# One layer block on one core: prologue and seams listed anew, a lead of 80, and the rotations' fourth layer behind the next pair's third

## The chip, the cores and the metric

The kernel runs on one core of one Trainium2 chip. The metric is the device time of one execution in microseconds (us). Engines are named as the profile names them: PE (TensorE, matmuls; PEld its weight loads), DVE (VectorE), ACT (ScalarE), POOL (GpSimd) and SP (SyncE, which here only issues DMAs). Each engine runs its own instructions in order; L633 is line 633 of the kernel before.

## What is computed

The input x is 2 x 2048 tokens of 256 features, in float32. Four residual layers follow each other: x + attention_a(layernorm(x)), x + ffn(layernorm(x)), x + attention_b(layernorm(x)), x + ffn(layernorm(x)), the two ffn with the same weights.

```python
# attention_a: 16 query heads of 16 features, 4 key/value heads, softmax over all 2048 keys
out = softmax(q @ k.T / 4) @ v;  return out @ Wo + bo
# ffn: three cycles over all tokens
gf = sigmoid(g3(gelu(g2(gelu(g1(x.mean(tokens)))))))          # once for each batch
for _ in range(3):
    tf = sigmoid(w4(gelu(w3(gelu(w2(gelu(w1(out))))))))       # layers of 256, 128, 64, 1
    out = out + (0.1 + range * (0.7*gf + 0.3*tf - 0.5) * 2) * twist(out)
# attention_b: linear attention, masked, no softmax: silu(q), silu(k) rotated, gate, norm, Wo
```

## The kernel before, in words

The 4096 tokens stand in SBUF as 8 blocks of 512 (blocks 0 to 3 are batch 0). The program is one list of instructions written by hand: Python generators are stepped at chosen places, and in_order (L136) ties each engine's instructions to the order of that list. So a line's place in the list is its place in the queue of every engine that it uses, SP's among them in the prologue (L627).

**Attention a** has 32 units, one for each block and group of four heads. For each unit, largest (L361) first finds the largest score of every query row: 64 steps of one matmul s (L376) and one DVE reduction (L380) over its 512 columns. After the last step nm (L390) joins them, ACT and POOL split it in two parts mt (L397, L398), and turn_maxima (L400) turns mt on DVE (L403) and sends it through DRAM to a_m with eight small DMAs. For every unit but the first and the last that turn stands behind the fourth step of the next unit (L386). Then the unit's 16 rounds kb (L638) compute the scores a second time, transposed: p is a score matmul (L648) and a matmul that subtracts the maxima (L652); ACT takes the exponential (L656); one round later weigh (L633) multiplies with the values into av. The steps of largest run ahead of the rounds. The prologue (L508 to L627) does LEAD = 74 steps before the first round; each round does four more (L659 to L673), and odd rounds of unit 0 one extra until six are done (L687, MORE), so that from round 11 on the lead is 80.

The prologue's other work is a generator, pieces (L593): block j's normalised tokens are turned (features), its keys and values made (keys, with transfers through DRAM that end in a_kP), its queries made for two halves (asked), its values turned (values). The loop at L623 takes one step and, at chosen n, one piece: 17 pieces at n = 4, 7, ..., 52 and five at n = 64, 66, ..., 72. A second generator, rows (L212), loads Wo and the output bias bo on SP (L216, L217, issued at L584); makes a diagonal matrix a_db of bo on POOL (L221); and multiplies it with ones on PE (a_pb, L226), which DVE copies to a_bo_row (L227). Its second step stands at L606, ahead of block 4's pieces, and its third at L619, behind them. a_bo_row is first read in unit 1 (L467).

**The rotations** (L773) are the ffn. Blocks go in pairs, four pairs by three cycles, so k = 0 to 11. For pair k, first(k, e) is layer 1 of one block (8 matmuls q1f, gelu on ACT to a1), second(k) layer 2 of both (8 matmuls q2f, gelu to a2), third(k) layer 3 of both (q3f, gelu to a3), and fourth(k) layer 4 and the update: two matmuls q4f, tanh on ACT, then for each block two DVE and two POOL multiplications and sums that rewrite zq (L852 to L864). Pair k + 4 reads that zq. In the last cycle (k of 8 and more) fourth is back (L886): the blocks are turned back to tokens on PE (trf) and added to xs by DVE (L879, L912). context (L777) is the gf network of one batch in four steps: gm on DVE (L781), p1f, p2f, p3f on PE with ACT between. fourth needs its result for its batch. rounds(f, n) (L1208) lists the steady part: even n is fourth(k-2), second(k-1), first(k, 0); odd n is third(k-1), first(k, 1), with k = n // 2.

**The seams.** Between the first rotations and attention b (L1300 to L1322) block 0's query, key, gates and values are made while pair 11 ends; each of query and key is a projection on PE, silu on ACT, products on POOL and a shuffle on DVE, and rotate adds the two parts on DVE (L1043). Between attention b and the second rotations (L1391 to L1409) the last block is normalised and turned (next_turn), and context(1) runs step by step (front1).

Of the kernel before, what the change touches and what calls it, by code (L numbers as in the profile page):

```python
# [20 lines left out]
NB = T // BLK  # L21
BPB = N // BLK
KB = N // P
# [44 lines left out]
def tile_hybrid(ctx: ExitStack, tc: tile.TileContext, x: bass.AP, consts: bass.AP, wa_d: bass.AP, wf_d: bass.AP, wb_d: bass.AP, out: bass.AP):  # L68
# [84 lines left out]
    def attention_a():  # L153
        with ExitStack() as st:
# [150 lines left out]
            def keys(j, ld):  # L305

                pk = psp.tile([P, BLK], F32, tag="p", name=f"pk{j}")
                for c in range(2):
                    mm(pk, wkv[:, c, :], planes[j][c], start=(c == 0), stop=(c == 1))
                kv = kvs[j] = ld.tile([P, BLK], F32, tag="kv", name=f"kv{j}")  # L310
                kh, kl = (ld.tile([64, BLK], d, tag=t, name=f"{t}{j}") for t, d in (("kh", F32R), ("kl", F32)))
                if j == 0:
                    halve(kh, kl, None, pk[0:64, :], bkv[0:64, :])
                    nc.scalar.activation(kv[64:P, :], pk[64:P, :], AF.Identity, bias=bkv[64:P, :])
                else:
                    nc.scalar.activation(kv, pk, AF.Identity, bias=bkv)
                    halve(kh, kl, kv[0:64, :], None, None)
                d = stored("dk", (kh, kl), (0, 0, 1, 1), nc.sync)
                return lambda: fetch([kP[p][:, j * BLK : (j + 1) * BLK] for p in range(2)], d)
# [41 lines left out]
            def largest():  # L361


                turning = []
                for u, (j, g) in enumerate(units):
                    k0 = (j // BPB) * N
                    qP = queries[u]
                    mx = sb.tile([P, KV, 4, 4], F32, tag="mx", name=f"mx{u}")
                    first = u == 0

                    def step(kb, qi, r):

                        pool, tag = (psp, "p") if first and (4 * qi + r) % 5 > 2 else (pss, "s")
                        s = pool.tile([P, BLK], F32, tag=tag, name=f"s{u}_{kb}_{qi}_{r}")
                        row = slice(64 * (r % 2), 64 * (r % 2) + 64)
                        mm(  # L376
                            s, qP[r // 2][row, qi * P : (qi + 1) * P],
                            kP[r // 2][row, k0 + kb * BLK : k0 + (kb + 1) * BLK], start=True, stop=True,
                        )
                        nc.vector.tensor_reduce(mx[:, r, qi : qi + 1, kb], s, AX.X, ALU.max)  # L380

                    for kb in range(4):
                        for qi in range(4):
                            for r in (0, 1, 3, 2):
                                step(kb, qi, r)
                                if (kb, qi, r) == (0, 0, 2) and turning:  # L386
                                    turning.pop()()
                                yield
                    nm = sb.tile([P, KV, 4], F32, tag="nm", name=f"nm{u}")
                    nc.vector.tensor_reduce(nm, mx, AX.X, ALU.max, negate=True)  # L390

                    mt = sb.tile([P, KV, 2, 4], F32, tag="mt", name=f"mt{u}")
                    if first:
                        nc.vector.tensor_copy(mt[:, :, 0, :].bitcast(F32R), nm)
                        nc.vector.tensor_tensor(mt[:, :, 1, :], nm, mt[:, :, 0, :], ALU.subtract)
                    else:
                        nc.scalar.copy(mt[:, :, 0, :].bitcast(F32R), nm)  # L397
                        nc.gpsimd.tensor_tensor(mt[:, :, 1, :], nm, mt[:, :, 0, :], ALU.subtract)  # L398

                    def turn_maxima(u=u, mt=mt):  # L400

                        mr = sb.tile([P, 32], F32, tag="mr", name=f"mr{u}")
                        turn = nc.vector.transpose(mr, mt.rearrange("p r i q -> p (r i q)"))  # L403
                        tc.keep_in_program_order(turn)
                        d = dram.tile([2 * KV, BLK], F32, tag="dm", name=f"dm{u}")
                        for i in range(4):
                            nc.sync.dma_start(
                                d.rearrange("r (q b x) -> (r q) b x", b=4, x=32)[:, i, :], mr[32 * i : 32 * i + 32, :]
                            )
                        for p in range(2):  # L410
                            for i in range(2):
                                nc.sync.dma_start(
                                    mrows[u % 2][p][64 * i : 64 * i + 2, :].bitcast(F32),
                                    d[4 * p + 2 * i : 4 * p + 2 * i + 2, :],
                                )

                    if first or u + 1 == len(units):
                        turn_maxima()
                    else:
                        turning.append(turn_maxima)  # L420
# [83 lines left out]
                        nc.vector.tensor_tensor(pair, pair, po.rearrange("p (t d) -> p t d", t=2), ALU.add)  # L504
                        yield


            LEAD, MORE, WARM = 64 + 10, 6, 6  # L508
            ahead = largest()
            begin = len(nc.cur_bb.bb.instructions)  # L510
            loads = ExitStack()
# [47 lines left out]
            second = keys(1, ld)  # L559
# [5 lines left out]
            third = keys(2, ld)  # L565
# [6 lines left out]
            third = keys(3, ld)  # L572
# [10 lines left out]
            more = rows()  # L583
            next(more)  # L584

            def memsets():
                for t in mrows[0] + mrows[1]:
                    nc.gpsimd.memset(t.bitcast(F32), 0.0)
                nc.gpsimd.memset(pick.bitcast(F32), 0.0)
                for p in range(2):  # L590
                    nc.gpsimd.memset(pick[64 * p : 64 * p + 2, :].bitcast(F32), 1.0)

            def pieces():  # L593

                memsets()
                look(4)
                values(3)
                for j in range(1, BPB):
                    for m in range(2):
                        asked(j, m)  # L600
                        yield
                        if (j, m) == (2, 0):
                            spread(4, ld, 0)
                next(more)
                for j in range(BPB, NB):
                    features(j, ld, 0)  # L606
                    if j + 1 < NB:
                        look(j + 1)
                    yield
                    keys(j, ld)()  # L610
                    if j + 1 < NB:
                        spread(j + 1, ld, 0)
                    yield
                    asked(j, 0)
                    yield
                    asked(j, 1)
                    values(j)
                    if j == BPB:
                        next(more)  # L619
                    yield  # L620

            rest = pieces()
            for n in range(4, LEAD):  # L623
                next(ahead)
                if (n % 3 == 1 and n < 55) or (n > 63 and n % 2 == 0):
                    next(rest, None)
            in_order(begin, (engines.DVE, engines.Activation, engines.Pool, engines.SP))  # L627

# [9 lines left out]
            for u, kb in ((u, kb) for u in range(len(units)) for kb in range(KB)):  # L638
# [45 lines left out]
                if kb > 1:  # L684
                    next(done, None)
                    next(norms, None)
                if kb % 2 == 1 and u * KB + kb < 2 * MORE:  # L687
                    next(ahead)
                if u % G == 1 and kb == 1 and G < u < 4 * G:
                    norms = norm(u // G - 1)  # L690
                if kb == 4 and u + 2 < len(units):
# [32 lines left out]
    def behind(tail):  # L724
# [483 lines left out]
        def rounds(f, n):  # L1208

            context, first, second, third, fourth, _ = f  # L1210
            k = n // 2
            if n % 2 == 0:
                if 0 <= k - 2:
                    fourth(k - 2)
                if 0 <= k - 1 < 12:
                    second(k - 1)
                if k < 12:
                    first(k, 0)
            else:
                if 0 <= k - 1:  # L1220
                    third(k - 1)
                if k < 12:
                    first(k, 1)

        f = rotations(0, sums0, False)
        context, first, second, third, fourth, _ = f
# [20 lines left out]
        front, front1, more = context(0), context(1), linear_weights()  # L1247
# [42 lines left out]
        next(front1)  # L1290
        first(4, 0)
        next(front1)
        fourth(2)
        aside = {10: more, 12: more}
        for n in range(9, 22):
            rounds(f, n)
# [3 lines left out]
        zero, one = blocks[0], blocks[1]  # L1300
# [11 lines left out]
        zero.turn()  # L1312
        third(11)
        zero.query()
        zero.rotate()
        zero.key()
        fourth(11, zero.rotate)
        zero.narrow()
        zero.gates()
        zero.keys_by_tokens()  # L1320
# [4 lines left out]
        context, first, second, third, fourth, turn_ahead = f  # L1325
# [70 lines left out]
        second(1)  # L1396
        fourth(0)
        first(2, 1)
        x.next_turn()
        third(1)  # L1400
        next(front1)
        fourth(1)
        next(front1)
        second(2)
        first(3, 0)
        next(front1)
        third(2)
# [9 lines left out]
        in_order(begin)  # L1417

    behind(attention_a())


# [115 lines left out]
```

## Time and profile before

| | |
|---|---|
| median of 3 runs | 2130.35 us (2127.65 to 2135.94) |
| the profiled execution | 2133.95 us, of which the profile's span is 2132.2 |
| prologue | 0 to about 107 us |
| 32 units of attention a | 107 to 1527 |
| first rotations, with the end of attention a | 1527 to 1697 |
| middle seam | 1697 to 1721 |
| attention b, with the start of the second rotations | 1721 to 1976 |
| last seam | 1976 to 2000 |
| second rotations | 2000 to 2132 |

A group's row gives line, engine, operation, output and inputs, count, then busy time, mean of one, and the idle time before with what ended it. The timeline gives start and length in us, and in brackets the idle time before a row and what released it. A row of stretches gives for each engine the busy us and the instructions; then PE's granted clock, where 1.00 is full speed, the share of the DMA engines, and GB/s. In the chain that ended last, a row is start, length and what ran; the whole chain is PE for 93% of the span and DVE for 3%.

### The profile page before, as it was taken

Reading aid. Unit: us, or ns where it says so; the run is one execution under the profiler, and the core shown is the slowest. Engines: PE = TensorE matmul, PEld = TensorE weight load, DVE = VectorE, ACT = ScalarE, POOL = GpSimd, SP = SyncE. Lnnn points to the kernel's source line nnn. Section 1 sums busy time; section 2 is a strip of 40 time slices with the busy share of each in tenths; the row PEclk is TensorE's granted clock in tenths of the full one; section 3 lists DMA queues with packets and bytes.
Section 4 is the critical chain, followed back from the end, with each engine's and each line's share of the span. In section 5 each row is a group of like instructions: output and inputs, shape, how many; then the busy total and the mean of one; then the engine's idle time right before and its main releaser. Section 6 shows DMA issues by size and latency. Waiting matters only on the chain.

```text
span 2132.2 us, 38745 instructions
## 1 busy us (share of the span) xinstructions
PE 2101.0 (99%) x14158; PEld 1018.7 (48%) x14158; DVE 1700.7 (80%) x3241; ACT 1427.6 (67%) x2787; POOL 355.6 (17%) x352
## 2 busy tenths in 40 slices
PE   9899999999999999999999999999999999999998
PEld 4344444444444444444444444444443567776434
DVE  7689998998999999899899899987134688886335
ACT  4377777777777877777777777777864445554443
POOL 3100000001001000000000000000135355551450
PEclk9799999999999999999999999999999999999999
DMA  6320110101101011010110101100100000000002
GB/s 204 92 88 10 49 37 17 47 10 47 37 19 37 18 49 39 18 38 20 47 37 20 37 19 48 38 18 8 52 1 1 0 2 1 2 1 2 0 0 79
DMA packets 59695, 68.71 MB, mean 32 GB/s; under 512 B 24944, under 2 KB 34032, under 8 KB 59248
## 3 DMA queue, kind: packets, MB, share of 16 engines
q1 hardware_dynamic: 58592, 64.79, 11.2%
q8 instruction: 111, 1.82, 0.4%
q10 hardware_dynamic: 720, 0.92, 0.1%
q14 instruction: 80, 0.66, 0.1%
q0 software_dynamic: 192, 0.52, 0.1%
HBM read 35.78 MB, written 26.21 MB: 29 GB/s over the span
## 4 chain that ended last, share of the span: by engine, by line
PE 93%; DVE 3%; issue 1%; ACT 1%; POOL 1%; DMA 1%; SPq 0%; DVEq 0%; POOLq 0%; ACTq 0%
PE av L633 24%; PE s L376 22%; PE p L648 11%; PE q1f L817 8%; PE p L652 7%; PE q2f L827 4%; PE pe L1117 2%; PE bpo L1143 2%; PE po L499 1%; PE pq L975 1%; PE pk L975 1%; PE pw L984 1%; PE pv L984 1%; DVE mx L380 1%; PE q3f L839 1%
## 5 line engine op out<-in xcount | busy, mean ns | idle before, releaser
L380 DVE TENSOR_REDUCE mx<-s 128x1 f32<-128x512 f32 x2048 | 1272.7, 683 | 110.7 <-PE s L376 106.4
L656 ACT ACTIVATE e<-p 128x512 f32<-128x512 f32 x2048 | 1057.7, 603 | 312.8 <-PE p L652 305.9
L376 PE MATMUL s<-a_kP,qP 64*128 64x512 f32 x2048 | 707.0, 471 | 4.8 <-DVE mx L380 2.8
L652 PE MATMUL p<-a_m,a_pick 64*128 64x512 f32 x2048 | 586.5, 415 | 0.0
L376 PEld LDWEIGHTS s<-a_kP,qP 64*128 64x128 f32 x2048 | 283.5, 184 | 567.4 <-DVE mx L380 550.8
L633 PE MATMUL av<-e,a_v 128*32 128x512 f32 x4096 | 546.8, 605 | 0.0
L648 PE MATMUL p<-qP,a_kP 64*128 64x512 f32 x2048 | 527.5, 394 | 2.5 <-ACT e L656 2.5
L648 PEld LDWEIGHTS p<-qP,a_kP 64*128 64x128 f32 x2048 | 286.9, 185 | 64.6 <-ACT e L656 25.5
L652 PEld LDWEIGHTS p<-a_m,a_pick 64*128 64x128 f32 x2048 | 284.6, 184 | 26.1
L817 PE MATMUL q1f<-zq,wf 128*128 128x512 f32 x384 | 175.7, 600 | 0.0
L633 PEld LDWEIGHTS av<-e,a_v 128*32 128x32 f32 x4096 | 81.0, 108 | 129.2 <-issue 121.2
L818 ACT ACTIVATE a1f<-q1f,wf 128x512 f32<-128x512 f32 x96 | 65.8, 686 | 102.2 <-PE q1f L817 99.0
L398 POOL TENSOR_TENSOR mt<-nm,mt 128x16 f32<-128x16 f32 x31 | 6.9, 221 | 736.3 <-ACT mt L397 736.3
L817 PEld LDWEIGHTS q1f<-zq,wf 128*128 128x128 f32 x384 | 70.5, 190 | 97.4 <-issue 84.9
L827 PE MATMUL q2f<-a1f,wf 128*128 128x512 f32 x192 | 90.7, 616 | 0.0
L1123 DVE TENSOR_TENSOR en<-pe,small 128x512 f32<-128x512 f32 x128 | 79.4, 683 | 11.3 <-PE pe L1117 11.2
L237 POOL TENSOR_TENSOR ql<-zq,qh 128x512 f32<-128x512 f32 x15 | 19.3, 1286 | 359.5 <-ACT qh L234 359.5
L858 DVE TENSOR_SCALAR cf<-cf,f_beta,alphaf 128x512 f32<-128x512 f32 x32 | 33.6, 1050 | 54.0 <-ACT cf L857 54.0
L862 POOL TENSOR_TENSOR tf<-cf,zq 128x512 f32<-128x512 f32 x32 | 56.6, 1768 | 93.5 <-DVE cf L858 93.1
L829 ACT ACTIVATE a2f<-q2f,wf 128x512 f32<-128x512 f32 x48 | 32.6, 685 | 53.3 <-PE q2f L827 53.3
L827 PEld LDWEIGHTS q2f<-a1f,wf 128*128 128x128 f32 x192 | 35.6, 195 | 45.8 <-issue 44.7
L864 POOL TENSOR_TENSOR zq<-zq,tf 128x512 f32<-128x512 f32 x32 | 56.8, 1776 | 2.5
(209 smaller groups left out, 1633.5 us busy)
## 6 DMA issues: line engine op xcount, KB each, us to landing
qP<-dq SPq DMA_DIRECT2D x64, 256.0 KB
dq<-qh SPq DMA_DIRECT2D x62, 128.0 KB
dq<-ql SPq DMA_DIRECT2D x62, 128.0 KB
a_kP<-dk SPq DMA_DIRECT2D x16, 256.0 KB
oc<-avs SPq DMA_DIRECT2D x128, 32.0 KB
sums<-dr SPq DMA_DIRECT2D x128, 32.0 KB
out<-xs SPq DMA_DIRECT2D x16, 256.0 KB
xs<-in_x SPq DMA_DIRECT2D x7, 512.0 KB
```

The costliest lines, as they stand in the source:

```text
L376: mm(s, qP[r // 2][row, qi * P : (qi + 1) * P], kP[r // 2][row, k0 + kb * BLK : k0 + (kb + 1) * BLK], start=True, stop=True,)
L380: nc.vector.tensor_reduce(mx[:, r, qi : qi + 1, kb], s, AX.X, ALU.max)
L633: mm(av[32 * r : 32 * r + 32, :], vA[:, units[u][0] // BPB * KB + kb, 32 * r : 32 * r + 32], es[r], start=(kb == 0), stop=(kb == KB - 1),)
L648: mm(t[r], kP[r // 2][row, k0 : k0 + P], qP[r // 2][row, :], start=True, stop=False)
L652: mm(t[r], pick[row, :], mrow[r // 2][row, :], start=False, stop=True)
L656: nc.scalar.activation(es[r], t[r], AF.Exp, scale=1.0 / HD**0.5)
L817: mm(q1, w1[:, c, m * P : (m + 1) * P], z[:, c, :], start=(c == 0), stop=(c == 1))
L818: nc.scalar.activation(a1[:, m, :], q1, AF.Gelu, bias=b1[:, m : m + 1])
L827: mm(q2, w2[:, c, :], a1[:, c, :], start=(c == 0), stop=(c == 1))
L862: nc.gpsimd.tensor_tensor(t1, cs, z[:, 0, :], ALU.mult)
L864: nc.gpsimd.tensor_tensor(z[:, 1, :], z[:, 1, :], t1, ALU.subtract)
L1123: nc.vector.tensor_tensor(self.ens[t][w], pes[w].rearrange("p (h n) -> p h n", h=4), const("triu").unsqueeze(1).to_broadcast([P, 4, P]), A ...
```

## The change

LEAD becomes 80, and the extra steps of unit 0 (MORE) go. The prologue's 22 pieces are spread anew: 19 at n = 4, 7, ..., 58 and three at n = 64, 66, 69; ten steps then stand alone. Both remaining steps of rows go into the last piece. The turn of a unit's maxima stands one reduction earlier. In rounds, and where the seams are written out, fourth(k) of the first two cycles stands behind third(k + 1) and not ahead of second(k + 1). In the middle seam block 0's key is projected between the two halves of fourth(11). In the last seam second(2) stands ahead of fourth(1), and next_turn behind third(1).

```diff
-                                if (kb, qi, r) == (0, 0, 2) and turning:
+                                if (kb, qi, r) == (0, 0, 3) and turning:
...
-            LEAD, MORE, WARM = 64 + 10, 6, 6
+            LEAD, WARM = 64 + 16, 6
...
-                next(more)
                 for j in range(BPB, NB):
                     features(j, ld, 0)
...
-                    if j == BPB:
+                    if j + 1 == NB:
+                        next(more)
                         next(more)
...
-                if (n % 3 == 1 and n < 55) or (n > 63 and n % 2 == 0):
+                if n % 3 == 1 and n < 61 or n in (64, 66, 69):
                     next(rest, None)
...
-                if kb % 2 == 1 and u * KB + kb < 2 * MORE:
-                    next(ahead)
...
-                if 0 <= k - 2:
+                if 0 <= k - 2 and k - 2 >= 8:
                     fourth(k - 2)
...
                     third(k - 1)
+                if 0 <= k - 2 < 8:
+                    fourth(k - 2)
...
         next(front1)
-        fourth(2)
         aside = {10: more, 12: more}
...
         zero.query()
+        def amid():
+            zero.rotate()
+            zero.key()
+        fourth(11, amid)
         zero.rotate()
-        zero.key()
-        fourth(11, zero.rotate)
...
         first(2, 1)
+        third(1)
         x.next_turn()
-        third(1)
         next(front1)
+        second(2)
         fourth(1)
         next(front1)
-        second(2)
         first(3, 0)
```

## The prediction

> **What bounds the kernel now.** I read the page first, then busy time by stage, the timelines of three places where TensorE (PE) stands still, and the chain that ended last. The page:
>
> ```profile
> PE 2101.0 (99%) x14158; PEld 1018.7 (48%) x14158; DVE 1700.7 (80%) x3241; ACT 1427.6 (67%) x2787; POOL 355.6 (17%) x352
> ...
> PEclk9799999999999999999999999999999999999999
> ```
>
> PE is the bound nearly everywhere; the digits of its granted clock name one place where it is not simply busy, slice 2 (53 to 107 us). By stage (columns: stretch, length, then busy us of PE, PEld, DVE, ACT, POOL, then the clock):
>
> ```profile
> 0.00:107.00 107.00, 94.84 (x290) 42.02 (x292) 72.26 (x182) 39.30 (x75) 28.78 (x49) 0.87 0.51 148
> 152.00:198.00 46.00, 46.00 (x344) 20.61 (x340) 42.74 (x72) 35.83 (x71) 0.22 (x1) 1.00 0.07 20
> 1600.00:1697.00 97.00, 97.00 (x298) 43.71 (x297) 51.15 (x120) 44.47 (x70) 45.24 (x33) 1.00 0.00 1
> 1697.00:1721.00 24.00, 20.66 (x118) 13.02 (x116) 21.83 (x56) 11.99 (x23) 10.40 (x8) 1.00 0.00 1
> 1976.00:2000.00 24.00, 21.24 (x56) 9.26 (x55) 12.86 (x26) 11.29 (x22) 14.08 (x10) 0.86 0.00 0
> ```
>
> The attention loop (152 to 198) and the rotations (1600 to 1697) are full: only shorter PE work helps there. Prologue, middle seam (1697 to 1721) and last seam (1976 to 2000) have idle PE, and two of them a lower clock.
>
> **The bias block.** Line 606 makes bo_row inside the prologue. Timeline of before:
>
> ```profile
> 54.61 0.46 PE L326 MATMUL pv<-small,kv 64*128 64x64 f32 x4
> 57.90 0.42 SPq L217 DMA_DIRECT2D a_bo<-in_wa  x1
> 59.62 0.76 POOL L221 TENSOR_TENSOR a_db<-small,a_bo 128x128 f32<-128x128 f32 x2 [23.14 <-DMA a_bo<-in_wa]
> 60.43 1.22 PE L226 MATMUL a_pb<-a_db,small 128*128 128x256 f32 x2 [5.37 <-POOL a_db L221]
> 61.69 0.42 DVE L227 COPY a_bo_row<-a_pb 128x256 f32<-128x256 f32 x1 [6.93 <-PE a_pb L226]
> ```
>
> POOL waits 23.14 us for the load of bo, at the end of SP's queue; PE waits 5.37 for POOL, DVE 6.93 for PE. Behind POOL's wait also stand kl (61.58) and the statistics of block 5. Then the clock:
>
> ```profile
> 56.00:58.00 2.00, 0.00 (x0) 0.00 (x0) 0.00 (x0) 0.00 (x0) 0.00 (x0) 0.76 0.41 119
> 70.00:72.00 2.00, 2.00 (x6) 0.59 (x5) 0.18 (x1) 0.96 (x2) 0.00 (x0) 0.83 0.00 0
> 86.00:88.00 2.00, 0.61 (x5) 0.27 (x4) 2.00 (x5) 0.00 (x0) 0.00 (x0) 0.94 0.32 36
> 100.00:102.00 2.00, 2.00 (x5) 0.36 (x3) 0.00 (x0) 0.61 (x1) 0.00 (x0) 0.65 0.00 0
> ```
>
> Full speed is 1.00 and the low state 0.50, so the means give the edges: half clock from 57.04 to 70.68 and from 87.76 to 101.40, 13.64 us each. The first follows the idle stretch; the second follows twelve reductions in a row (from 82.4) in which PE only trickles. In them four matmuls take 3.60 to 3.78 us instead of 1.98.
>
> **Prologue after, step by step.** The block goes to the last piece, where bo is long there. From 55.07 on nothing then waits, and pieces and steps go on as just before: one cycle of a block (12 steps, four pieces) took 45.43 to 55.7, that is 10.3 us (DVE: 12 reductions of 0.62, a look of 2.0, a cast 0.4). Blocks 5 and 6 end at 76.3. Turning block 7 and the six steps to n = 64 are DVE's: 3.6, to 79.9. Then PE's pk 1.98, two pq 3.96, values 0.46, pb 0.6 (half of 1.22, at full clock) and five scores 1.2: 88.1. Ten steps are left plus the loop's first ones; DVE paces them at 0.62, and the first p (L648) starts with reduction 78 at 94.4. Before it started at 106.99. Lower bound: DVE alone from 54.76, 48 reductions 29.8, looks 4.4, casts 1.3, maxima 0.8, copy 0.4: 91.5. Upper bound: one more spell of half clock over these 8.2 us of PE work: 100.5. What is late next is DVE. SP's queue keeps its order: the keys' transfers of block 4 still start at 58.43 and take some 5.4 us a block (two issues 1.1 ahead of kl, 62.87 to 67.14 behind it), but they feed only the second batch, units 16 on. POOL has the sums for bo (0.76) at about 86, behind kl of block 7, and nothing waits there.
>
> **Lead of 80.** The six extra steps at odd kb (L687) leave the loop. There av starts at 111.66 for kb 1 and 143.06 for kb 11, 3.14 us a round; in the full stage 181.50, 184.21, 186.91, 2.705 a round. After: av of kb 1 at 94.4 + 4.4, of kb 11 27.05 later: 125.9 against 143.1, **17.2 us** for both together. But the ten bare steps (PE 0.22 of each 0.62) are like those before 87.76, so I expect half clock at the loop's start: 2 us lost (bounds 0 and 6.8, half of 13.64). Net **-15.2**, from -8 to -18.
>
> [...]
>
> **Turn of the maxima one reduction earlier** (L386). nm ends 0.75 us before mt is ready (188.26 to 189.01); the transpose now comes 2.1 after nm instead of 2.6. DVE still doesn't wait. Its eight DMAs come 0.6 earlier on an SP queue with nothing else to issue then, and nothing waited for a_m. 0 (bounds -0.2 and +0.2 in each of 31 units).
>
> **Fourth behind third** (L1210, 11 rounds). One round of before, and one behind transposes, in the chain:
>
> ```profile
> 1638.39 3.63 PE q2f L827 x8
> 1642.03 3.43 PE q1f L817 x8
> 1646.47 3.63 PE q1f L817 x8
> 1651.16 3.63 PE q2f L827 x8
> ...
> 1665.45 3.44 PE q2f L827 x8
> ```
>
> Round 12.77 = 3.63 + 3.43 + 1.0 (q3) + 3.63 + 1.06 (q4). Eight matmuls behind the narrow q3 or q4 take 0.2 more than behind full ones (3.44). With q4 behind q3 one such change goes: 0.2 x 11 = **-2.2** (bound 0, if q3 to q4 costs as much). Cover: q2's second half needs a1 0.69 after PE and has 1.7 of its first half. The new z is needed after first 3.6, second 3.4, first 3.4, q3 and q4 2.1, first 3.6 and second 3.4, 19.5 us, and takes 10 (two ACT 1.3, a DVE 0.6, POOL 4 x 1.77, gaps 1); no wait. At the start of the first rotations fourth(2) only changes places with q3.
>
> **Middle seam.** The key's projection moves between the halves of fourth(11). DVE works the same list (swaps, 3.74 twice, rotations) with the second 3.74 ahead of the key's rotation instead of behind; PE waited there for DVE (pv 1.47, pt 0.72). rotk, at 1717.3 before, comes at 1716.9 to 1717.9. 0, bounds -1.7 and +3.7.
>
> **Last seam.** Timeline of before:
>
> ```profile
> 1990.00 1.13 PE L852 MATMUL q4f<-a3f,wf 64*128 64x512 f32 x4 [0.79 <-ACT a3f L841]
> 1991.82 0.15 DVE L781 TENSOR_REDUCE gmf<-sums 128x2 f32<-128x8 f32 x1
> 1993.10 1.01 PE L786 MATMUL p1f<-gmf,wf 128*128 128x1 f32 x4 [1.97 <-DVE gmf L782]
> 1993.98 6.28 PE L827 MATMUL q2f<-a1f,wf 128*128 128x512 f32 x8
> ```
>
> gm stands in DVE's queue behind fourth(0), which waits for POOL; PE idles 0.79 and 1.97, the clock falls (1992.4 to 1999.2) and q2 takes 6.28. After, second(2) comes before fourth(1): from 1987.17 q3 1.0, turn 1.0, q2 3.5, q4 1.06, p1 0.4 end at 1994.1; gm (1993.05) is there at 1993.7. first(3, 0) starts at 1994.1 instead of 2000.09: **-5.9** (bounds -2.8, the two waits alone, and -6.5). PE is full from there to 2116, so it stays.
>
> **Sum.** -15.2 - 2.2 - 5.9 = -23.3. The profiled execution took 2133.95 (span 2132.2 and 1.75 around it): 2110.6. The median shown, 2130.35, lies 3.6 lower, so **2107**.
>
> **Rivals.** (A) The forecast, 2107 (2100 to 2112): chance 0.55. (B) The half clock lasts four windows as at 57 and 87, at the loop's start (6.8 instead of 2) or over block 7's pieces (6): 2112, both 2118; for it the two rows, against it the loop, which once lost the clock, at 333, and had it back 3.4 us later; 0.22. (C) The wait for bo was hiding another, so that prologue and loop start give half, 8: 2114, and without the last seam 2120; for it the crowded DMA (share 0.51), against it that everything loaded by 57 is read after it; 0.18, half of it above 2119.7. (D) Slower: the transpose, now after three reductions, waits for POOL in each unit. It decides from mt later than 2.1 us after nm (0.75 seen); with POOL's bias add of 2.4 ahead of it, 3.15, DVE stops 1.05 x 31 = 33 us: 2140. Against it: that add follows mt (146.50 after 146.32); 0.05.
>
> About 0.5% (10.7 us) is what a measurement can tell from no change. Faster 0.55 + 0.22 + 0.09 = 0.86, within 0.09, slower 0.05. Range 2100 to 2120: A, B and most of C.
>
> **What would show it.** Right: no PE gap at 55 to 60, clock 1.00 until about 91, first L648 at 94.4, av every 2.7 from kb 1, q2 at 3.44 in the rotations, no p1 wait. Wrong: L648 after 100, a transpose waiting for POOL, or q1f waiting for zq.

## The result, and the profile after

| | median us | executions |
|---|---|---|
| before | 2132.62 | 4 (2127.65 to 2135.94) |
| changed | 2108.61 | 4 (2107.98 to 2109.11) |

The ratio is 0.9889 (95%: 0.9867 to 0.9911): 24.0 us less, where 23.3 were forecast (2107, 2100 to 2120). The profiled execution took 2107.98, of which its span is 2106.2; so 26.0 us lie between the two spans. The page of the changed kernel:

```profile
PE 2085.9 (99%) x14158; PEld 1011.4 (48%) x14158; DVE 1697.6 (81%) x3241; ACT 1427.5 (68%) x2787; POOL 355.2 (17%) x352
...
PEclk9999999999999999999999999999999999999999
```

PE does the same 14158 matmuls in 15.1 us less, and the 7 in the clock's digits is gone. Busy time by stage (prologue to the first p, middle seam, last seam up to first(3, 0)):

```profile
0.00:94.07 94.07, 89.27 (x297) 39.39 (x297) 75.57 (x189) 39.80 (x76) 28.81 (x49) 0.99 0.60 174
1679.00:1703.00 24.00, 21.20 (x113) 13.22 (x113) 19.80 (x57) 12.44 (x24) 9.96 (x8) 1.00 0.00 1
1956.00:1974.73 18.73, 18.73 (x58) 7.91 (x57) 8.57 (x20) 11.12 (x21) 8.35 (x7) 1.00 0.00 0
```

The prologue's clock went from 0.87 to 0.99, the last seam is full at 1.00, and the middle seam still has 2.8 us of idle PE. The bias block and the first p in the timeline (what is line 648 before is 647 here; later lines shift by two or three):

```profile
84.71 0.75 POOL L221 TENSOR_TENSOR a_db<-small,a_bo 128x128 f32<-128x128 f32 x2
87.38 0.70 PE L226 MATMUL a_pb<-a_db,small 128*128 128x256 f32 x2
88.11 0.42 DVE L227 COPY a_bo_row<-a_pb 128x256 f32<-128x256 f32 x1 [1.52 <-PE a_pb L226]
...
94.07 1.22 PE L647 MATMUL p<-qP,a_kP 64*128 64x512 f32 x2
```

POOL's wait of 23.14 and PE's of 5.37 are gone, and no wait of that kind took their place (DVE waits 1.52 for a_pb): the first p starts at 94.07 instead of 106.99. The clock, by stretches of 2 us:

```profile
90.00:92.00 2.00, 1.80 (x4) 0.71 (x4) 2.00 (x4) 0.00 (x0) 0.00 (x0) 0.82 0.23 44
96.00:98.00 2.00, 2.00 (x12) 1.16 (x10) 1.83 (x4) 1.52 (x3) 0.00 (x0) 0.50 0.95 364
98.00:100.00 2.00, 2.00 (x17) 0.73 (x13) 1.94 (x4) 1.82 (x4) 0.00 (x0) 0.97 0.66 273
```

By the same reading as in the prediction, one spell of half clock is left, from 91.28 to 98.12 (6.84 us), where there were two of 13.64. It begins in the bare steps, and DVE is nearly full in it (1.80 or more of each 2.00). A round of the rotations, in the chain that ended last:

```profile
1613.94 1.06 PE q4f L849 x4
1615.00 3.63 PE q1f L814 x8
1618.63 3.43 PE q2f L824 x8
```

q2 now takes 3.43 behind q1 instead of 3.63 behind q4; a round takes 12.56 (q4 at 1601.38, 1613.94 and 1626.51) where it took 12.77. The last seam in the timeline:

```profile
1972.29 0.15 DVE L778 TENSOR_REDUCE gmf<-sums 128x2 f32<-128x8 f32 x1
1973.20 1.13 PE L849 MATMUL q4f<-a3f,wf 64*128 64x512 f32 x4
1974.26 0.61 PE L783 MATMUL p1f<-gmf,wf 128*128 128x1 f32 x4
1974.73 3.68 PE L814 MATMUL q1f<-zq,wf 128*128 128x512 f32 x8
```

gm is ready while q4 runs, so p1 has no wait for DVE (1.97 before), and the clock holds. first(3, 0) starts at 1974.73 instead of 2000.09.

The whole path between the two traces, by how much earlier the same instruction comes in the changed kernel: 17.0 at the av of round 11 (126.09 for 143.06) and 17.45 some units later; 18.9 behind 337, because the profiled execution of before lost the clock at 333 and that of the changed kernel did not; 18.2 at the end of attention a; then 0.7 in the first rotations, 0.65 in the middle seam, 5.84 in the last seam and 0.6 in the second rotations. The sum is 26.0.

### The profile page after: what moved, and what is told of

It reads as the page before. It is cut to its first block, busy times and chain, and to the rows that moved or that the text cites. A ratio compares the mean times of both kernels' runs of the same rounds, so it can differ in the third digit from the quotient of the medians.

```text
span 2106.2 us, 38754 instructions
## 1 busy us (share of the span) xinstructions
PE 2085.9 (99%) x14158; PEld 1011.4 (48%) x14158; DVE 1697.6 (81%) x3241; ACT 1427.5 (68%) x2787; POOL 355.2 (17%) x352
## 4 chain that ended last, share of the span: by engine, by line
PE 95%; DVE 2%; DMA 1%; ACT 1%; issue 0%; POOL 0%; SPq 0%; DVEq 0%; ACTq 0%; POOLq 0%
PE av L632 24%; PE s L376 23%; PE p L647 12%; PE q1f L814 8%; PE p L651 7%; PE q2f L824 4%; PE pe L1114 2%; PE bpo L1140 2%; PE po L499 1%; PE pq L972 1%; PE pw L981 1%; PE pv L981 1%; PE pk L972 1%; PE q3f L836 1%; PE pq L336 1%; DVE mx L380 1%
## 5 line engine op out<-in xcount | busy, mean ns | idle before, releaser
L491 POOL TENSOR_TENSOR oc<-oc,sums 128x512 f32<-128x512 f32 x16 | 20.6, 1288 | 209.6 <-DMA sums<-dr 138.2
```

## The experiments

The experiments come in three groups, each with its own executions of the kernel before: medians 2130.12 (e1 to e4), 2130.41 (e5 to e8) and 2132.84 (e9 to e12). Ratios are to these. "After" is the changed kernel.

**e1: after, with the bias block back in its two old places.**

```diff
+                next(more)
                 for j in range(BPB, NB):
...
-                    if j + 1 == NB:
-                        next(more)
+                    if j == BPB:
                         next(more)
```

> The changed kernel with the bias block alone put back to where it stood, ahead of and behind block 4's pieces. If the wait for bo and the half clock behind it cost about 10 us in the prologue (my theory), the first shifted score comes near 104 instead of 94.1, PE stands idle some 5 us near 55 again, and the time is about 2118. If the lead and the new spacing made the gain and the wait hid something else (rival), it stays below 2112.

2118.33 us, ratio 0.9946 (0.9927 to 0.9965); first p at 104.36. The wait is back, in the timeline of e1:

```profile
61.34 0.75 POOL L221 TENSOR_TENSOR a_db<-small,a_bo 128x128 f32<-128x128 f32 x2 [23.67 <-DMA a_bo<-in_wa]
```

So 11.8 us of the gain are left without the block's move, and by the medians 12.4 of the 24.2 that e5 shows hang on it. By the traces it is less: av of round 11 comes at 136.44 in e1 and at 126.09 in after, 10.35 later, and the distance is 10.3 at the end too.

**e2: before, with the block alone moved to the last piece** (the same lines, the other way round).

> The kernel before with the bias block alone moved to the last piece. My theory: the first shifted score at about 97 instead of 107, time some 10 us below the kernel before (near 2122). Rival (the wait hid another): not more than 3 us below it.

2118.70, ratio 0.9949 (0.9933 to 0.9964): 11.4 less, more than expected, with the first p at 93.53. In its trace the bare steps at the end of the old spacing cost less clock than they did in before. Stretches of e2:

```profile
78.00:80.00 2.00, 1.90 (x5) 0.82 (x6) 2.00 (x4) 0.00 (x0) 0.00 (x0) 0.72 0.81 260
82.00:84.00 2.00, 2.00 (x12) 1.13 (x12) 1.06 (x3) 0.95 (x2) 0.00 (x0) 0.92 0.05 6
```

Half clock from 78.88 to 82.32: one stretch of 3.4 us, where before had 13.64 behind the same twelve reductions.

**e3: before, with bo loaded early on ACT's queue and the block left in its place.**

```diff
-                nc.sync.dma_start(bo, wa_d[:, slice(*_WA["bo"])])
...
+            nc.scalar.dma_start(bo, wa_d[:, slice(*_WA["bo"])])
```

> The kernel before with the bias block in its old place, but bo loaded at the start from ACT's queue. If only the lateness of the load was the trouble, this is as fast as moving the block, near 2122 with the first shifted score at about 97. If the place itself costs (POOL, PE and DVE in one chain amid the pieces), the gain is under half of that, above 2127.

2121.19 (2116.10 to 2124.38), ratio 0.9958 (0.9942 to 0.9974); profiled at 2116.85, with a_pb at 56.28 without a wait and the first p at 93.64. In these traces the place was not the trouble, the late load was: either cure brings the first p to 93.6. But the executions fall into two groups: 2116.1 and 2116.9 at a mean clock of 0.997, and 2120.3 to 2124.4 at 0.994 to 0.995. The trace is of the faster group, and e2 has no such slower group; whether the block in its old place costs clock in the others is open.

**e4: before, with idle matmuls on PE ahead of a_pb**, to tell the half clock behind the wait from the wait itself.

```diff
+                warm = psp.tile([P, BLK], F32, tag="p", name="warm")
+                for _ in range(6):
+                    mm(warm, still[:, 0:P], still, start=True, stop=True)
                 pb = psp.tile([P, BLK], F32, tag="p", name="a_pb")
```

> The kernel before with twelve idle matmuls (5.1 us, their result unused) ahead of the bias block's on PE: the wait stays, but PE is not idle in it. If the half clock behind the wait costs by itself (my theory: 4 to 5 of the 10 us), the clock stays at 1.00 from 55 to about 85, and the time is near 2127. If what counts is the wait alone, the time stays at 2131 or more although the clock stays up.

2131.01, ratio 1.0002 (0.9991 to 1.0013). In its trace the clock is 1.00 from 54 to 84, and the way from a_pb to the score of step 40 takes 6.92 (62.07 to 68.99) instead of 10.85 (60.43 to 71.28), so there the half clock behind the wait cost 3.9. (The idle matmuls themselves hold a_pb up by 1.1: a_db is done at 60.94.) The first p comes at 101.05, 5.9 us earlier, also because the spell of half clock at the bare steps lasts 6.8 there and not 13.64. But that execution took 2127.24, near the lowest of the ten (2125.84 to 2134.31), and the median gains nothing: that the half clock behind the wait costs 4 to 5 us by itself is not borne out by the times. What the other executions lost instead can't be read from one trace; this stays open.

**e5 and e12: after again**, as marks for the others.

> The changed kernel once more, as the mark for the three beside it: 2108.6 by its first runs (2108 to 2109).

> The changed kernel again, as the mark for the other three: the time of e5, within 1 us (2105 to 2107.5).

2106.24 (2104.85 to 2108.32), ratio 0.9886 (0.9871 to 0.9900), and 2108.33 (2108.22 to 2109.45), ratio 0.9887 (0.9870 to 0.9904): within 2.1 us of each other on different chips, 24.2 and 24.5 below their own before.

**e6: after, with the last seam as before.**

```diff
         first(2, 1)
-        third(1)
         x.next_turn()
+        third(1)
         next(front1)
-        second(2)
         fourth(1)
         next(front1)
+        second(2)
```

> The changed kernel with the last seam alone as it was. My theory (gm behind fourth(0) stops PE, and the clock falls): 5.8 us slower than the changed kernel, near 2114.4, with half clock for some 3.4 to 6.8 us in the seam. [...] Rival (PE only waits somewhere else): within 1 us of it.

2111.99, ratio 0.9913 (0.9898 to 0.9928): 5.75 slower than e5. Timeline of e6:

```profile
1973.66 0.88 PE L783 MATMUL p1f<-gmf,wf 128*128 128x1 f32 x4 [1.97 <-DVE gmf L779]
1974.40 5.09 PE L824 MATMUL q2f<-a1f,wf 128*128 128x512 f32 x8
```

The wait of 1.97 returns to the hundredth, and with it a loss of the clock: q2 takes 5.09 instead of 3.60. But not all of the 5.75 is the seam. In its trace e6 is 1.54 behind e5 where first(2, 1) begins, part of it through half clock in the middle seam (1697.4 to 1700.8), which the edit doesn't touch, and 6.06 behind at first(3, 0): 4.5 for the seam. The other traces with the old seam say why that is less than the 5.84 between before and after. In e3 the clock stays at 1.00 through it, with the same wait in front of p1:

```profile
1979.38 3.68 PE L827 MATMUL q2f<-a1f,wf 128*128 128x512 f32 x8
```

From first(2, 1) to first(3, 0) it takes 13.46 there; 15.16 in e2 and 15.14 in e6, with 3.4 of half clock; 16.35 in e4 and 16.46 in before, with 6.8; and 10.63 in the new order. So the two waits cost 2.8, the first 3.4 us of half clock 1.7 more and the next 3.4 another 1.2 to 1.3, and how much of it comes differs between executions of the same seam.

**e7: after, with the fourth layer ahead of the second again, in rounds and at the start of the first rotations.**

```diff
-                if 0 <= k - 2 and k - 2 >= 8:
+                if 0 <= k - 2:
...
-                if 0 <= k - 2 < 8:
-                    fourth(k - 2)
...
         next(front1)
+        fourth(2)
```

> The changed kernel with fourth ahead of second again in the rounds, the seams as changed. My theory (0.2 us for each change between narrow and full matmuls): rounds of 12.77 instead of 12.57, 1.5 to 2.2 us slower in all, near 2110.4. Rival (the order does nothing for PE): within 0.5 us.

2108.35, ratio 0.9894 (0.9879 to 0.9908): 2.1 slower than e5 by the medians, 2.4 by the spans. The spans hold more than the edit, because e7's profiled execution lost the clock twice in attention a (half clock from 315 to 319 and from 677 to 680). Between the same instructions the first and the second rotations take 0.7 longer each, 1.4 together. The chain of e7 shows the old price:

```profile
1618.70 1.06 PE q4f L849 x4
1619.76 3.63 PE q2f L824 x8
```

**e8: after, with the turn of the maxima behind the fourth reduction again.**

```diff
-                                if (kb, qi, r) == (0, 0, 3) and turning:
+                                if (kb, qi, r) == (0, 0, 2) and turning:
```

> The changed kernel with the turn of the maxima behind the fourth reduction again. The two traces drift apart by 0.03 us a unit against the earlier turn, so by that theory 0.9 us faster, near 2107.7. Rival (the earlier transfers of the maxima help): slower by up to 1 us.

2105.71, ratio 0.9882 (0.9866 to 0.9899): 0.5 faster than e5, which the medians can't tell from nothing. The traces can't either. An nm stands at 213.9 in both, and at the first q3 of the round at 1598 e8 is 0.72 ahead (1598.18 for 1598.90), 0.02 us for each unit; but the same program drifts by more: from the av of round 11 to the last av it takes 1384.98 in after, 1383.50 in e5 and 1385.07 in e12, without half clock in between, 1382.73 in e8, and 1383.49 in e10, which has e8's turn. In the changed kernel PE's next weight load of a score waits for the turn (mr) in each unit, but the same load waits as long in e8, for a reduction. First after, then e8:

```profile
259.68 0.19 PEld L376 LDWEIGHTS s<-a_kP,qP 64*128 64x128 f32 x2 [0.84 <-DVE mr L403]
259.46 0.18 PEld L376 LDWEIGHTS s<-a_kP,qP 64*128 64x128 f32 x2 [0.84 <-DVE mx L380]
```

So no price of the earlier turn is shown.

**e9: after, with the lead and the pieces' spacing as before.**

```diff
-            LEAD, WARM = 64 + 16, 6
+            LEAD, MORE, WARM = 64 + 10, 6, 6
...
-                if n % 3 == 1 and n < 61 or n in (64, 66, 69):
+                if (n % 3 == 1 and n < 55) or (n > 63 and n % 2 == 0):
...
+                if kb % 2 == 1 and u * KB + kb < 2 * MORE:
+                    next(ahead)
```

> The changed kernel with the lead and the spacing of the pieces as before (74 steps and six extra ones in the loop), the bias block still in the last piece. If most of the prologue's gain is the block and the lead adds the rest: first p at about 93.5, as in e2, rounds of 3.14 up to kb 11, so some 5 to 6 us later than the changed kernel from kb 11 on, 2112 (half clock behind the bare steps at the end of the prologue may add or spare 2). If the lead is worth nothing: within 1 us of the changed kernel. If the two parts only work together: above 2116.

2112.57 (2111.30 to 2117.02), ratio 0.9911 (0.9895 to 0.9927): 4.2 slower than e12. Its prologue is that of e2, step for step, but its trace shows another clock. Stretches of e9:

```profile
78.00:80.00 2.00, 1.72 (x4) 0.97 (x5) 2.00 (x5) 0.00 (x0) 0.00 (x0) 0.52 0.81 230
90.00:92.00 2.00, 2.00 (x4) 0.46 (x3) 0.00 (x0) 0.25 (x1) 0.00 (x0) 0.57 0.00 0
```

Half clock from 78.08 to 91.72, 13.64 us, and the first p at 98.19 instead of 93.53. (It also lost the clock at 27 and at 505, for 3.4 us each.) That execution took 2116.27 at a mean clock of 0.994, and one more took 2117.02; the three at 0.997 to 0.998 took 2111.3 to 2112.6. So one list of instructions has two outcomes some 5 us apart; in the traces of e2 and e9 the difference at the first p is whether the clock comes back after one stretch of 3.4 us or after four.

**e10: after, with the last three pieces at n = 63, 68 and 73, and e8's edit**, meant to beat both kernels.

```diff
-                if n % 3 == 1 and n < 61 or n in (64, 66, 69):
+                if n % 3 == 1 and n < 61 or n in (63, 68, 73):
```

> The changed kernel with its last three pieces at n = 63, 68 and 73, so that fewer steps stand bare, and with the turn of the maxima behind the fourth reduction as before. If DVE's idle time of 1.8 in the prologue's end can be filled and the single spell of half clock there goes: 1 to 2 us for the prologue and 0.5 for the turn, 2 us faster than the changed kernel. If DVE's list alone sets the first p: only the 0.5.

2113.62 (2111.07 to 2117.76), ratio 0.9911 (0.9896 to 0.9927): 5.3 slower than e12, with the first p at 98.50. The theory that DVE's list alone sets the first p falls here. Stretches of e10:

```profile
82.00:84.00 2.00, 0.00 (x0) 0.00 (x0) 1.93 (x4) 0.00 (x0) 1.72 (x3) 0.98 0.60 130
86.00:88.00 2.00, 2.00 (x3) 0.76 (x3) 0.60 (x2) 0.00 (x0) 0.00 (x0) 0.50 0.31 103
```

Timeline of e10:

```profile
84.27 1.39 PE L376 MATMUL s<-a_kP,qP 64*128 64x512 f32 x2 [3.16 <-DVE mx L380]
```

Behind step 64 DVE joins and turns the maxima of the first unit (nm, mt and mr, 81.59 to 83.64). With the piece moved from n = 64 to 63 PE has nothing to do meanwhile and waits 3.16; the clock falls at 83.92, the next piece's matmuls take twice their time (four in 3.78 for 1.98), and now DVE waits 3.53 for PE. A second spell follows the last bare steps (97.56 to 104.40). In after PE is nearly full from 56 to 88 (1.77 or more of each 2.00), and its only spell begins where DVE sets the pace.

**e11: after, with the middle seam as before.**

```diff
-        def amid():
-            zero.rotate()
-            zero.key()
-
-        fourth(11, amid)
         zero.rotate()
+        zero.key()
+        fourth(11, zero.rotate)
```

> The changed kernel with the middle seam as before: rotate, key, fourth(11, rotate). By the two traces 0.65 us slower than the changed kernel; by the prediction's sum 0 (bounds from 3.7 faster to 1.7 slower).

2108.86, ratio 0.9887 (0.9872 to 0.9902): 0.5 above e12, within the spread. In the traces the way from the last q3 to the first pe is 21.96 in e11 and 21.29 in e12, so the new order gains 0.67.

Put back one at a time, the parts cost by the medians 12.4 (block), 4.2 (lead and spacing), 5.75 (last seam), 2.1 (fourth layer), 0.5 (middle seam) and -0.5 (turn), 24.5 together, against 24.2 and 24.5 for the whole change. That this comes out so closely is partly chance. Between the same instructions of the traces the block costs 10.35, the last seam 2.8 to 5.8, the fourth layer 1.4 and the middle seam 0.67, and the lead and spacing 3.4 or 8.1 at round 11, by the prologue as e2 ran it (129.54) or as e9's profiled execution did (134.19). The parts are real, but neither their exact sizes nor that they are independent of each other is shown.

## Why the prediction was right, step by step

- **Bias block and lead, 17.2 forecast:** 17.0 at round 11 and 17.45 behind it. First p forecast at 94.4, measured 94.07; av of round 11 forecast at 125.9, measured 126.09. (The 4.4 taken from the first p to the first av was short: it is 4.67 in before and 4.96 in after.) The step behind it, that DVE is what is late next, holds in e2, e3 and after, which all reach the first p between 93.5 and 94.1. It holds only as long as PE keeps its clock in the pieces and has work beside the maxima: e9's trace and e10 come at 98.
- **Half clock at the loop's start, 2 forecast:** the step that was mis-sized. No run shows the 2 itself, the author's estimate between the bounds of 0 and 6.8. The spell came where it was expected (91 to 98), 6.84 us long, but cost 0.2 to 0.5 in this trace: 17.2 - 17.0 at round 11, and the start of p had already come 0.3 early. In the bare steps DVE sets the pace (2.00 busy of each 2.00 from 90 to 94), so a PE at half speed loses little there. Behind the first p it loses more: e5 has the same list and 6.8 of half clock too, but 0.9 later (92.14 to 98.97), and its way from the first p to the av of round 11 takes 32.72 instead of 32.02; in e7, where the spell ends at 96.71, it takes 31.61. So the price of one and the same spell varies by 1.1, with where it happens to fall. Where PE is the bound, as in the last seam, the price of a spell was about half of its length (1.7 for the first 3.4).
- **Fourth behind third, 2.2 forecast:** also mis-sized; 1.3 by adding up the two traces (0.7 and 0.6), 1.4 by those of e5 and e7 (2.1 by their medians). Ten rounds, five in each rotations, gain 0.2 each as forecast, but in both the way into the new order costs 0.1 and the way out 0.2: there first(10, 0) takes 0.2 longer.
- **Last seam, 5.9 forecast:** 5.84 by the traces of before and after, 5.75 by e6's median, 4.5 by e6's trace. (The forecast's own figures, 2000.09 - 1994.1, give 6.0.) The mechanism was right (gm late, two waits, then the clock); that the size came out so well is owed to the profiled execution of before, from which the forecast was made and which had 6.8 us of half clock there. With the clock kept, as in e3, the same order costs 2.8, the lower bound of the forecast.
- **Middle seam, 0 forecast:** 0.65 gained. PE now waits 1.38 once for the key's rotation instead of 1.47 and 0.72.
- **Turn of the maxima, 0 forecast:** nothing else is shown. The two traces drift apart by 0.7 from 337 to the end of attention a, but the changed kernel's own traces differ there by 1.5. The reason given holds: DVE waits for mt once in after, for 0.6, as in before.

**Rivals.** B (a spell of four windows at the loop's start, that is of 13.64 us, as the two of before): it lasted 6.84, and B's price of half the length would have been 3.4; measured 0.5 at most in this trace, because DVE sets the pace for much of it. C (another wait hidden behind the load): the first p would have come near 100; it came at 94.07, and e3 shows the same with the block in its place. D (the transpose waiting for POOL): no such wait in each unit of the trace, and e8 is 0.5 faster by its median, not 33.

The agreement with the median has some luck in it: 1.5 to 1.8 were taken off too much for the clock and 0.65 was not seen in the middle seam, against 0.9 too much for the fourth layer and 0.7 of drift in attention a. And 1.4 of the 26.0 between the spans is a spell of half clock at 333 that before's profiled execution had and the changed kernel's had not; it belongs to no part of the change.

## What to carry to other kernels

A load that is last in its queue and first in another engine's list stopped three engines in a row here (POOL for 23.14, DVE for 6.93, PE for 5.37); look for the longest wait of an engine that is otherwise idle (POOL, 17% busy) and see who stands behind it. A second cost follows on PE: in these traces half clock came with stretches in which PE idled or trickled (5.37 idle at 55 in before, 0.61 busy of 2.00 at 86), and it cost most in work that PE bounds (1.7 for the first 3.4 in the last seam, 0.2 to 0.5 for the 6.84 in after from 91.28 on), so fill the stretches ahead of PE's heavy work and leave the thin ones where another engine sets the pace. And when the executions of one kernel spread by several us, read their mean granted clock beside their times before you price an edit from one trace, and compare the time between the same two instructions rather than whole spans.

## What the runs showed of the hardware

- **Spells of half clock came in multiples of 3.41 us**, within 0.03: 3.44 (e2), 6.84 (after), 6.80 and 6.84 (e10), 10.2 (e1, behind the wait) and 13.64 (twice in before, once in e9). How soon full clock came back was not one figure: in e9 PE was busy 2.00 of 2.00 from 80 on and stayed at half clock to 91.72, while e2, with the same list up to there and PE at 2.00 of 2.00 from 80 on too, was back at 82.32. What decides it is not shown.
- **The spread of before goes with its clock.** Over its executions beside e9 the time rises with falling mean clock, from 2128.22 at 0.994 to 2134.81 and 2135.82 at 0.990. By arithmetic 0.001 of the mean is 4.3 us of half clock, or 2.1 us lost where PE is the bound; the 0.004 here would be 8.5, measured 6.6 to 7.6. The changed kernel (0.995 to 0.997 over its twelve executions) lies between 2104.85 and 2109.45. Not all of that is clock: the drift of 1.5 in attention a between its traces, told at e8, comes without half clock, and its cause is open.
- **Behind the narrow q3 or q4 eight matmuls took 0.2 longer:** those of layer 1 or 2 take 3.63 there and 3.43 behind each other, in the rounds of the first two cycles of both kernels (first(10, 0) takes 3.64 behind q2 in after).
- **Half clock can follow a short wait.** In attention a PE stands still for 0.85 at three places, because ACT is late with an exponential, and nowhere else from 140 to 1500 for more than 0.4; the first of the three in before stands in the row below, the others are near 513 and 693. In the fourteen traces that makes 42 such waits, and behind four of them (one in before, two in e7, one in e9) half clock of 3.4 us follows within 3 us, at a cost of 1.2 to 1.45; no other half clock lies between round 11 and the end of attention a. Behind the other 38 nothing happens. Why it follows some and not others is open. The change leaves these waits as they were.

```profile
331.80 0.97 PE L648 MATMUL p<-qP,a_kP 64*128 64x512 f32 x2 [0.85 <-ACT e L656]
```
